# Graph attention with residual and layer norm: ScalarE's work in a step ordered by need, and steps between the load, the codes and the maxima of an edge list

## The chip, the cores and the metric

The kernel runs on one core of a Trainium2 chip. The time is that of the device for one execution, in microseconds (us). The engines are TensorE (PE in the profile, its weight loads PEld), VectorE (DVE), ScalarE (ACT), GpSimd (POOL) and SyncE (SP), which issues most of the DMAs. Each engine works through its own instructions in the order in which they were written, and waits for other engines by semaphores.

## The reference

```python
def ref(x, adj, Wq, bq, Wk, bk, Wv, bv, Wo, bo):      # x: (16, 1024, 512), adj: (1024, 1024) of 0 and 1
    q, k, v = ((x @ W + b).reshape(16, 1024, 8, 64) for W, b in ((Wq, bq), (Wk, bk), (Wv, bv)))
    scores = einsum('bqhd,bkhd->bhqk', q, k) / 8 + (1 - adj) * -1e9
    out = einsum('bhqk,bkhd->bqhd', softmax(scores), v).reshape(16, 1024, 512)
    return layernorm(x + out @ Wo + bo)
```

All in float32. The adjacency is the same for all 16 batch entries and sparse: the chance of an edge falls with the numbers of its two nodes, so the first rows have many edges and the last few.

## The kernel before

The scores of absent edges vanish in the softmax, so the kernel works on edges alone. The 1024 queries of a batch entry are 8 tiles of 128. For each tile, `edges(t)` makes lists from the adjacency once, before or beside the first batch entry. A tile's edges are then worked off in *blocks*: a block gives each of the 128 partitions one edge. `OWN[t]` blocks hold edges of the partition's own query; what queries have beyond that is spread over `BLOCKS[t]` more blocks, whose results are added up by a product with a 0/1 matrix. That is 36 blocks per batch entry, 576 in all.

One *step* n of the main loop does one piece of several blocks: `gather(n + 8)` fetches rows of k and v (and of q) by an indirect DMA on POOL; `products(n + 4)` and `scores(n + 4)` on DVE form q k for 8 heads; `exponentials(n + 3)` on ACT (L720); `weigh(n + 1)` multiplies v by the exponentials, called p v here, either in one DVE operation (L734) or in eight ACT operations, one per head (L730; `by_act` says which); then `add_own(n)` (DVE, L746) adds p v to the tile's sum, or `add_up(n)` does it by two products on PE (L755, L756). When a tile's blocks are through, `normalise` divides by the denominators (DVE, L762 to L769), PE transposes, and `finish` multiplies by Wo, adds x (DVE, L641) and takes the layer norm: the sum of squares on ACT (L648, behind `centre` on DVE, L644), a small root on POOL (L651 to L653), the scaled output on ACT (L656) and its store on SP (L657).

Beside this, PE makes q, k and v of a later batch entry, in units that fill the step up to a share of time: x is transposed (`pxT`, copied to `xT` by ACT, L434), q = x Wq (`pq`, L459; evicted by DVE, L486), and k and v of two tiles at once from seven block products with sums of x and of the weights (`x`, `p6`, `p7`, `z`, `p4`; L575), evicted by ACT (`e`, L588; `kv`, L492) and DVE (L591 to L607). PE's results lie in 4 PSUM banks of the tag `fill` and a few of their own. For a bound on the scores, `norm` squares each q and k (L471, eight ACT operations per tile, one per head, each with a read-out of its accumulator).

The order is written out by hand: the program is recorded step by step, and every engine keeps that order. `later(k, fn)` puts a piece of work into the plan of step n + k. In a step, ACT gets first the exponentials, then the plan's pieces in the order in which they were put there (copies from PSUM, squares, L648, L656), then p v:

```python
                for fn in plan.pop(n, ()):
                    fn()
                if 0 <= n + 1 < total and by_act(n + 1):
                    weigh(n + 1)
```

There are 34 steps before step 0 (n from -34). In them the weights are loaded (`loads`, one piece per step up to each `yield`), the first k and v are made, and the edge lists are begun: `edges(t)` starts in step `EDGES_FROM[t]`. It loads 128 rows of the adjacency (`a`, DMA on SP, L330), multiplies them by column numbers on POOL (`codes`, L332), and one step later sums and checks `a` on ACT (L339 to L341) and begins to take the eight largest codes at a time on DVE (L343, L345). `a`, `codes` and the k and v tiles share 5 buffers of the tag `kv`.

Of the kernel before, what the change touches and what calls it, by code (L numbers as in the profile page):

```python
# [13 lines left out]
OP = mybir.AluOpType  # L14
# [19 lines left out]
ROWS = 3  # L34
EARLY = 10
LEAD_IN = 34
EDGES_FROM = (-32, -16, -12, -8, -4, 0, 5, 10)

PRODUCT = 0.86
SUM = 0.87  # L40
# [3 lines left out]
P = 128  # L44
# [103 lines left out]
def kernel(  # L148
# [34 lines left out]
    nc = tc.nc  # L183
    B, N, D = x.shape
# [26 lines left out]
    def load_w(t, w):  # L211
        nc.scalar.dma_start(t, w.rearrange("(c p) e -> p c e", p=P))

    with ExitStack() as main:
# [16 lines left out]
        place = one.tile([P, N], F32, name="place")  # L231
# [30 lines left out]
        def loads():  # L262

            load_w(W["q"], wq)
            broadcast(bq_bc, bq)
            nc.vector.tensor_scalar(bq_bc, bq_bc, scale, None, op0=OP.mult)
            yield

            B12[0] = work.tile([P, 2, D], F32, tag="kv", name="b12", bufs=5)
            load_w(B11, wk[0:HD2, :])  # L270
            load_w(B21, wk[HD2:D, :])
            load_w(B12[0], wv[0:HD2, :])
            load_w(B22, wv[HD2:D, :])
            yield
            load_w(W["o"], wo)
            yield
            nc.vector.tensor_tensor(T1, B12[0], B11, op=OP.subtract)
            yield
            nc.vector.tensor_tensor(T2, B22, T1, op=OP.subtract)
            nc.vector.tensor_tensor(T3, B22, B12[0], op=OP.subtract)  # L280
            nc.vector.tensor_tensor(T4, B21, T2, op=OP.subtract)
            yield
            nc.vector.tensor_scalar(before, place[:, 0:P], -1.0, query[:, 0:1], op0=OP.add, op1=OP.is_gt)
            yield
            for i in range(ROWS):
                nc.scalar.dma_start(kv_rows[i][N:N + 1, 0:D], zero)
            broadcast(bo_bc, bo)
            yield
            nc.scalar.dma_start(bias_rows[0:NPAIR, :], bq.rearrange("(c p) -> c p", p=P))
            nc.scalar.dma_start(bias_rows[NPAIR:, :], bk.rearrange("(c p) -> c p", p=P))  # L290
            nc.scalar.dma_start(bv_rows, bv.rearrange("(c p) -> c p", p=P))

        def bias_setup():
            bk_bc = work.tile([P, D], F32, tag="y", name="bk_bc", bufs=4)
            broadcast(bk_bc, bk)
            yield
            n8 = small.tile([P, HEADS], F32, name="bk_norms")
            nc.vector.tensor_tensor(bk_bc, bk_bc, bk_bc, op=OP.mult)
            nc.vector.tensor_reduce(n8, bk_bc.rearrange("p (h d) -> p h d", d=HD), axis=AX.X, op=OP.add)
            nc.vector.tensor_reduce(bk_norm, n8, axis=AX.X, op=OP.max)  # L300
            yield
            pb = fill_psum("pb")
            nc.tensor.transpose(pb[:, 0:2 * NPAIR], bias_rows, ident[:2 * NPAIR, :2 * NPAIR])
            nc.tensor.transpose(pb[:, 2 * NPAIR:3 * NPAIR], bv_rows, ident[:NPAIR, :NPAIR])
            yield
            nc.vector.tensor_copy(bias_qk, pb[:, 0:2 * NPAIR])
            bv_col = one.tile([P, NPAIR], F32, name="bv_col")
            nc.vector.tensor_copy(bv_col, pb[:, 2 * NPAIR:3 * NPAIR])
            bvb = work.tile([P, NPAIR, P], F32, tag="y", name="bvb", bufs=4)
            nc.vector.tensor_copy(bvb, bv_col[:, :, None].to_broadcast([P, NPAIR, P]))  # L310
            yield
            pb = fill_psum("pb3")
            for c in range(NPAIR):
                nc.tensor.matmul(pb, bvb[:, c, :], W["o"][:, c, :], start=(c == 0), stop=(c == NPAIR - 1))
            yield
            nc.vector.tensor_tensor(bo_bc, pb, bo_bc, op=OP.add)

        now, plan, urgent = [0], {}, []  # L320

        def later(k, fn):
            plan.setdefault(now[0] + k, []).append(fn)

        def edges(t):
            nb, J, K = BLOCKS[t], DEGREE[t], OWN[t]
            a = work.tile([P, N], F32, tag="kv", name=f"a_{t}", bufs=5)
            nc.sync.dma_start(a, adj[ds(t * P, P), :])  # L330
            v = work.tile([P, N], F32, tag="kv", name=f"codes_{t}", bufs=5)
            nc.gpsimd.tensor_tensor(v, a, place[:, 0:N], op=OP.mult)  # L332
            st = small.tile([P, 4], F32, name="est")
# [5 lines left out]
            nc.scalar.activation(a, a, AF.Copy, accum_out=deg)  # L339
            nc.scalar.activation(a, a, AF.Square, bias=neg_one, scale=2.0)  # L340
            nc.scalar.activation(a, a, AF.Square, bias=neg_one, accum_out=check[:, t:t + 1])  # L341
            for r in range(J // 8):
                nc.vector.max(out=kl[:, ts(r, 8)], in_=v)  # L343
                if r < J // 8 - 1:
                    nc.vector.scalar_tensor_tensor(  # L345
                        v, v, kl[:, r * 8 + 7:r * 8 + 8], v, op0=OP.is_lt, op1=OP.mult
                    )
                    yield
# [117 lines left out]
        def norm(b, t, i, s):  # L466
            if t == 0 and i == 0:
                NRM[b] = work.tile([P, 2, NT, HEADS], F32, tag="nrm", name=f"nrm_{b}", bufs=2)
            for h in range(HEADS):
                sq = work.tile([P, HD], F32, tag="sq", name=f"sq_{b}_{t}_{i}_{h}", bufs=2)  # L470
                nc.scalar.activation(sq, s[:, ts(h, HD)], AF.Square, accum_out=NRM[b][:, i, t, h:h + 1])  # L471

        def pair(b, j):
# [8 lines left out]
            def out_q(i, p):  # L482

                assert gathered[0] >= NB * (b - ROWS + 1)
                q = work.tile([P, D], F32, tag="q", name=f"q_{b}_{tt[i]}", bufs=2)
                nc.vector.scalar_tensor_tensor(q, p, scale, bq_bc, op0=OP.mult, op1=OP.add)  # L486
                nc.sync.dma_start(q_rows[b % ROWS][ds(tt[i] * P, P), :], q)
                later(1, lambda: norm(b, tt[i], 0, q))

            def out_k(i, p):  # L490
                kv = new_kv(i)
                nc.scalar.copy(kv[:, 0:D], p)  # L492
                later(1, lambda: norm(b, tt[i], 1, kv[:, 0:D]))

            def out_v(i, p):
                nc.scalar.copy(KV[b, tt[i]][:, D:], p)
# [99 lines left out]
            def out_k1():  # L596
                kv = KV[b, tt[1]]
                nc.vector.tensor_tensor(kv[:, 0:D], R["p4"], R["g"], op=OP.add)
                send(1)
                later(1, lambda: norm(b, tt[1], 1, kv[:, 0:D]))  # L600

            def out_v1():
                nc.vector.tensor_tensor(new_kv(1)[:, D:], R["z"], R["g"], op=OP.add)
# [30 lines left out]
        def finish(b, t):  # L634

            def out(p):
                OT.pop((b, t))
                y = Y[b, t]

                st = small.tile([P, 5], F32, name="stats", bufs=6)  # L640
                nc.vector.scalar_tensor_tensor(y, p, 1.0, y, op0=OP.mult, op1=OP.add, accum_out=st[:, 0:1])  # L641

                def centre():
                    nc.vector.tensor_scalar(st[:, 1:2], st[:, 0:1], -1.0 / D, None, op0=OP.mult)  # L644

                def spread():
                    sq = work.tile([P, D], F32, tag="ysq", name=f"ysq_{b}_{t}", bufs=1)
                    nc.scalar.activation(sq, y, AF.Square, bias=st[:, 1:2], accum_out=st[:, 2:3])  # L648

                def root():  # L650
                    nc.gpsimd.tensor_scalar(st[:, 2:3], st[:, 2:3], 1.0 / D, EPS, op0=OP.mult, op1=OP.add)  # L651
                    nc.gpsimd.tensor_tensor(st[:, 3:4], st[:, 2:3], neg_half, op=OP.pow)  # L652
                    nc.gpsimd.tensor_tensor(st[:, 4:5], st[:, 3:4], st[:, 1:2], op=OP.mult)  # L653

                def norm_out():
                    nc.scalar.activation(y, y, AF.Identity, bias=st[:, 4:5], scale=st[:, 3:4])  # L656
                    nc.sync.dma_start(out_ap[b, ds(t * P, P), :], y)  # L657
                    del Y[b, t]

                later(1, centre)  # L660
                later(1, spread)
                later(2, root)
                later(4, norm_out)

            out_ap = out_dram
            return product(f"po_{b}_{t}", lambda: OT[b, t], W["o"], out)


# [53 lines left out]
        def by_act(n):  # L722
            b, t, i = blocks[n]
            return 0 < i < OWN[t] or ((b == B - 1 or i >= OWN[t]) and n % 2 == 0)
# [102 lines left out]
        prep = {}  # L827
        for t in range(NT):
            prep.setdefault(EDGES_FROM[t], []).append(edges(t))
        prep.setdefault(8 - LEAD_IN, []).append(bias_setup())  # L830
        preps = [loads()]
        prep.setdefault((B - 1) * NB, []).append(guard())
        with tc.manual_schedule():
# [9 lines left out]
            for t in range(3):  # L843
                load_x(0, t)
            n = -LEAD_IN
            while n < total or plan or urgent or done or finishing:
                now[0] = n
                if n < 0:
                    share = LEAD_SHARE if n > -LEAD_IN else TRANSPOSE * 1.5
# [19 lines left out]
                    normalise(*blocks[n - 1][:2])  # L869
                for fn in plan.pop(n, ()):  # L870
                    fn()
                if 0 <= n + 1 < total and by_act(n + 1):
                    weigh(n + 1)
                credit += share
                if 0 <= n < total and blocks[n][2] >= OWN[blocks[n][1]]:
                    add_up(n)
# [66 lines left out]
```

## Time and profile before

| | |
|---|---|
| median of 3 runs | 2289.22 us (2287.42 to 2289.9) |
| the profiled execution | 2296.11 us, span of its instructions 2294.3 us |
| mean granted clock of TensorE | 0.969 |
| PE busy | 2100.7 us, 92% of the span |
| DVE busy | 1874.1 us, 82% |
| ACT busy | 1642.8 us, 72% |
| POOL busy | 1286.8 us, 56% |
| 16 DMA engines | 578.00 MB, mean 252 GB/s |

A row of the timeline is: start, duration, engine, line, operation, out<-in, and in brackets the engine's idle time before it and what ended that. A row of waits is: engine, what it was about to do, what it waited for; total us, times, longest. A row of a stretch is: from:to, length, the busy time of PE, PEld, DVE, ACT and POOL with their instructions, the granted clock, the busy share of the DMA engines and GB/s. A row of a group of instructions ends with the number, the busy time, the mean ns of one, and the idle time before them by what ended it. The end of a PE product is modelled, so two products that follow each other overlap in these rows; the distance of their starts is the time that one takes.

### The profile page before, as it was taken

What the parts mean: (1) busy time and instruction counts of PE and PEld (TensorE: products, weight loads), DVE (VectorE), ACT (ScalarE), POOL (GpSimd) and SP (SyncE); (2) the same over time, 40 slices, a digit from 0 to 9 for tenths busy, and PEclk for the clock granted to TensorE, in tenths of its full rate; (3) what the DMA queues carried; (4) which work ended last, traced back from release to release, by engine and by line L of the source; (5) the groups of instructions that cost most, each with busy time, mean ns of one, the idle gap of its engine ahead of it and who ended that gap; (6) DMA issues with size and microseconds to landing.
All of it is one profiled execution on the core that took longest, in us unless ns stands there. A gap on an engine that the chain in (4) does not pass through costs nothing. (4 is left out here: it accounts for less than half of the span.)

```text
span 2294.3 us, 29416 instructions
## 1 busy us (share of the span) xinstructions
PE 2100.7 (92%) x5933; PEld 1033.0 (45%) x5933; DVE 1874.1 (82%) x3596; ACT 1642.8 (72%) x8100; POOL 1286.8 (56%) x1366
## 2 busy tenths in 40 slices
PE   7977888989999999999999999999999999999655
PEld 3433434444444444444454444444444444544322
DVE  5678978778887988879888887888788888978665
ACT  3556667587877778676877867687876878687655
POOL 2034455555656565665656555565656566575673
PEclk9989999999999999999999999999999999999868
DMA  4256868687887878787887878788787878778773
GB/s 170 92 191 207 262 217 284 223 266 269 286 283 249 292 257 293 242 278 253 275 289 269 283 235 283 251 285 283 247 289 246 300 260 287 260 258 279 228 240 114
DMA packets 216716, 578.00 MB, mean 252 GB/s; under 512 B 33727, under 2 KB 33739, under 8 KB 216526
## 3 DMA queue, kind: packets, MB, share of 16 engines
q0 software_dynamic: 102144, 331.89, 45.8%
q1 hardware_dynamic: 111776, 239.16, 28.5%
q10 hardware_dynamic: 2606, 4.99, 0.7%
q14 instruction: 141, 1.16, 0.1%
q8 instruction: 49, 0.80, 0.1%
HBM read 474.75 MB, written 134.26 MB: 265 GB/s over the span
## 5 line engine op out<-in xcount | busy, mean ns | idle before, releaser
L689 POOL DMA_INDIRECT kvg<-kv_rows,key_row x576 | 652.3, 1132 | 656.4 <-ACT pv L720 193.3
L730 ACT ACTIVATE pv<-kvg,pv 128x64 f32<-128x64 f32 x2592 | 651.5, 336 | 0.0
L459 PE MATMUL pq<-wq,xT 128*128 128x512 f32 x1024 | 492.0, 604 | 12.8 <-ACT xT L434 5.6
L459 PE MATMUL po<-wo,oT 128*128 128x512 f32 x1024 | 476.0, 605 | 1.7 <-DVE y L641 1.7
L710 DVE TENSOR_REDUCE s<-qk 128x8 f32<-128x512 f32 x576 | 392.0, 681 | 6.4
L684 POOL DMA_INDIRECT qg<-q_rows,query_row x240 | 269.1, 1121 | 91.2 <-issue 64.3
L746 DVE TENSOR_TENSOR pv<-pv,pv 128x520 f32<-128x520 f32 x208 | 153.4, 738 | 196.1 <-ACT pv L730 182.3
L459 PEld LDWEIGHTS po<-wo,oT 128*128 128x128 f32 x1024 | 197.9, 195 | 227.7 <-issue 209.1
L471 ACT ACTIVATE sq<-q 128x64 f32<-128x64 f32 x1024 | 245.7, 242 | 62.5 <-DVE q L486 50.1
L459 PEld LDWEIGHTS pq<-wq,xT 128*128 128x128 f32 x1024 | 191.9, 194 | 200.3 <-issue 170.1
L706 DVE TENSOR_TENSOR qk<-qt,kvg 128x512 f32<-128x512 f32 x336 | 245.7, 731 | 3.4 <-DMA kvg<-kv_rows,key_row 2.6
L575 PE MATMUL x<-b,xT 128*128 128x512 f32 x504 | 240.5, 600 | 7.4 <-ACT e L588 7.4
L471 ACT ACTIVATE sq<-kv 128x64 f32<-128x64 f32 x1024 | 245.0, 242 | 2.5 <-ACT sq L471 0.9
L720 ACT ACTIVATE pv<-s,absent 128x8 f32<-128x8 f32 x336 | 97.2, 294 | 198.3 <-DVE o L763 124.5
L575 PE MATMUL pp<-t,s 128*128 128x512 f32 x504 | 237.2, 593 | 0.0
L648 ACT ACTIVATE ysq<-y,stats 128x512 f32<-128x512 f32 x128 | 92.1, 720 | 180.7 <-DVE stats L644 163.0
L755 PE MATMUL sum<-pv,sums 128*128 128x256 f32 x480 | 155.7, 407 | 68.8 <-ACT pv L730 45.4
L632 POOL TENSOR_TENSOR y<-y,bo_bc 128x512 f32<-128x512 f32 x128 | 170.0, 1328 | 57.2 <-DMA y<-in_x_dram 56.1
L471 ACT ACTIVATION_READ_ACCUMULATOR sq<-q 128x1 f32 x1024 | 192.9, 188 | 0.0
L471 ACT ACTIVATION_READ_ACCUMULATOR sq<-kv 128x1 f32 x1024 | 192.7, 188 | 0.0
L706 DVE TENSOR_TENSOR qk<-qg,kvg 128x512 f32<-128x512 f32 x240 | 182.1, 759 | 6.1 <-DMA kvg<-kv_rows,key_row 5.9
L734 DVE TENSOR_TENSOR pv<-kvg,pv 128x512 f32<-128x512 f32 x252 | 177.0, 702 | 0.0
(144 smaller groups left out, 2954.8 us busy)
## 6 DMA issues: line engine op xcount, KB each, us to landing
kv_rows<-kv SPq DMA_DIRECT2D x128, 512.0 KB
x<-in_x_dram SPq DMA_DIRECT2D x128, 256.0 KB
q_rows<-q SPq DMA_DIRECT2D x128, 256.0 KB
qt<-q_rows SPq DMA_DIRECT2D x128, 256.0 KB
y<-in_x_dram SPq DMA_DIRECT2D x128, 256.0 KB
out_dram<-y SPq DMA_DIRECT2D x128, 256.0 KB
kvg<-kv_rows,key_row POOLq DMA_INDIRECT x576
a<-in_adj_dram SPq DMA_DIRECT2D x8, 512.0 KB
```

The lines of the kernel that those rows point to most:

```text
L459: nc.tensor.matmul(p, lhs()[:, ts(c, P)], w[:, c, :], start=(c == 0), stop=(c == NPAIR - 1))
L471: nc.scalar.activation(sq, s[:, ts(h, HD)], AF.Square, accum_out=NRM[b][:, i, t, h:h + 1])
L575: nc.tensor.matmul(R[bank], l[:, ts(c, P)], right[:, c, :], start=(first and c == 0), stop=(c == 1), skip_group_check=True,)
L632: later(2, lambda: nc.gpsimd.tensor_tensor(Y[b, t], Y[b, t], bo_bc, op=OP.add))
L684: nc.gpsimd.indirect_dma_start(out=QG[n], out_offset=None, in_=q_rows[b % ROWS], in_offset=bass.IndirectOffsetOnAxis(ap=query_row[:, g:g + ...
L689: nc.gpsimd.indirect_dma_start(out=KG[n], out_offset=None, in_=kv_rows[b % ROWS], in_offset=bass.IndirectOffsetOnAxis(ap=key_row[:, g:g + ...
L706: nc.vector.tensor_tensor(QK[n], q, KG[n][:, 0:D], op=OP.mult)
L710: nc.vector.tensor_reduce(S[n], QK.pop(n).rearrange("p (h d) -> p h d", d=HD), axis=AX.X, op=OP.add)
L730: nc.scalar.activation(pv[:, ts(h, HD)], v[:, ds(D + h * HD, HD)], AF.Copy, scale=pv[:, D + h:D + h + 1])
L734: nc.vector.tensor_tensor(pv[:, 0:D].rearrange("p (h d) -> p h d", d=HD), v[:, D:].rearrange("p (h d) -> p h d", d=HD), pv[:, D:, None].to ...
L746: nc.vector.tensor_tensor(PV[b, t], PV[b, t], pv, op=OP.add)
L755: nc.tensor.matmul(PSUM[b, t][:, 0, 0:HD2], m, pv[:, 0:HD2], **kw)
```

## The change

ACT's work in a step is put in another order. The squares of q and k, L648 and L656 go into a second plan, `rest`, which is emptied at the step's end; p v by ACT stands before it and is that of block n + 2 instead of n + 1. DVE's p v stays at n + 1. In `edges`, three steps lie between the load of `a` and the codes, and one between ACT's sums and the first maxima; `EDGES_FROM` is set for that: all lists but the first are loaded four steps earlier than before, their codes and sums are made one step earlier, and their maxima begin in the same step; the first list is loaded one step earlier, and its codes, sums and maxima come two to three steps later. In `loads` and for `bias_setup` some pieces change their step.

```diff
-EDGES_FROM = (-32, -16, -12, -8, -4, 0, 5, 10)
+EDGES_FROM = (-33, -20, -16, -12, -8, -4, 1, 6)
...
             load_w(B22, wv[HD2:D, :])
-            yield
+            for _ in range(3):
+                yield
             load_w(W["o"], wo)
+            for i in range(ROWS):
+                nc.scalar.dma_start(kv_rows[i][N:N + 1, 0:D], zero)
...
+        def later_last(k, fn):
+            rest.setdefault(now[0] + k, []).append(fn)
...
             nc.sync.dma_start(a, adj[ds(t * P, P), :])
+            for _ in range(3):
+                yield
             v = work.tile([P, N], F32, tag="kv", name=f"codes_{t}", bufs=5)
             nc.gpsimd.tensor_tensor(v, a, place[:, 0:N], op=OP.mult)
...
             nc.scalar.activation(a, a, AF.Square, bias=neg_one, accum_out=check[:, t:t + 1])
+            yield
             for r in range(J // 8):
...
-                later(1, lambda: norm(b, tt[i], 0, q))
+                later_last(1, lambda: norm(b, tt[i], 0, q))
...
-                later(1, spread)
+                later_last(1, spread)
                 later(2, root)
-                later(4, norm_out)
+                later_last(4, norm_out)
...
                 for fn in plan.pop(n, ()):
                     fn()
-                if 0 <= n + 1 < total and by_act(n + 1):
-                    weigh(n + 1)
+                if 0 <= n + 2 < total and by_act(n + 2):
+                    weigh(n + 2)
+                for fn in rest.pop(n, ()):
+                    fn()
```

The two other calls of `norm`, for k, change in the same way. From line 317 on, a line has a number that is 5 to 8 higher after the change (L720 becomes L726, L730 L736, L755 L761).

What this moves on ACT in the steady steps, here in steps 236 and 237, which begin with the exponentials of blocks 239 and 240 (tiles are named with their numbers: `pv_238` is p v of block 238, `sq_7_6_0_0` the square of head 0 of q in tile 6 of batch entry 7, `sq_7_6_1_0` that of k; seven more follow each). Before:

```order
L720 ACTIVATE pv_239_10779<-s_239_10756 128x8
L471 ACTIVATE sq_7_6_0_0_10790,nrm_7_9765<-q_7_6_10763 128x64
...
L492 COPY kv_7_6_10806<-x_7_3_10698 128x512
L720 ACTIVATE pv_240_10817<-s_240_10788,absent_107 128x8
L656 ACTIVATE y_5_6_10161<-y_5_6_10161,stats_10686 128x512
L471 ACTIVATE sq_7_6_1_0_10837,nrm_7_9765<-kv_7_6_10806 128x64
...
L730 ACTIVATE pv_238_10745<-kvg_238_10562,pv_238_10745 128x64 x8
```

After, on the same engine:

```order
L726 ACTIVATE pv_239_10779<-s_239_10764 128x8
L498 COPY kv_7_6_10790<-x_7_3_10706 128x512
L736 ACTIVATE pv_238_10753<-kvg_238_10562,pv_238_10753 128x64 x8
L477 ACTIVATE sq_7_6_0_0_10802,nrm_7_9773<-q_7_6_10771 128x64
...
L726 ACTIVATE pv_240_10825<-s_240_10788,absent_107 128x8
L662 ACTIVATE y_5_6_10169<-y_5_6_10169,stats_10694 128x512
L477 ACTIVATE sq_7_6_1_0_10845,nrm_7_9773<-kv_7_6_10790 128x64
```

The p v of block 238 has moved from behind the second step's squares to the first step, behind its copy and ahead of both sets of squares.

On SP, where the first k and v of batch entry 1 are stored (`mean_0` is the row of entry 0 that the first gathers wait for). Before:

```order
L330 DMA a_3_922<-in_adj_dram 128x1024
L487 DMA q_rows_1_114<-q_1_0_929 128x512
L524 DMA kv_rows_0_110<-mean_0_1001 1x512
L423 DMA x_1_5_1008<-in_x_dram 128x512
L423 DMA x_1_6_1012<-in_x_dram 128x512
L678 DMA qt_0_0_1027<-q_rows_0_113 128x512
L487 DMA q_rows_1_114<-q_1_1_1082 128x512
L501 DMA kv_rows_1_111<-kv_1_1_1014 128x1024
L501 DMA kv_rows_1_111<-kv_1_0_932 128x1024
L330 DMA a_4_1098<-in_adj_dram 128x1024
```

After, on the same queue:

```order
L333 DMA a_4_932<-in_adj_dram 128x1024
L493 DMA q_rows_1_114<-q_1_0_934 128x512
L530 DMA kv_rows_0_110<-mean_0_970 1x512
L429 DMA x_1_5_977<-in_x_dram 128x512
L429 DMA x_1_6_981<-in_x_dram 128x512
L684 DMA qt_0_0_1029<-q_rows_0_113 128x512
L493 DMA q_rows_1_114<-q_1_1_1089 128x512
L507 DMA kv_rows_1_111<-kv_1_1_983 128x1024
L507 DMA kv_rows_1_111<-kv_1_0_937 128x1024
L333 DMA a_5_1108<-in_adj_dram 128x1024
```

The load of `a_4` has moved from behind these eight DMAs to the place ahead of them, where `a_3` was; its codes on POOL stand behind four gathers of block rows, as before behind five.

On ACT at the start, around the first edge list (`a_0`) and the copies of x^T. Before:

```order
L471 ACTIVATE sq_0_0_0_7_206,nrm_0_191<-q_0_0_175 128x64
L339 ACTIVATE a_0_184,est_188<-a_0_184 128x1024
L340 ACTIVATE a_0_184<-a_0_184,neg_one_84 128x1024
L341 ACTIVATE a_0_184,check_108<-a_0_184,neg_one_84 128x1024
L471 ACTIVATE sq_0_1_0_0_231,nrm_0_191<-q_0_1_208 128x64
...
L434 COPY xT_0_2_247<-pxT_0_2_211 128x512
L434 COPY xT_0_3_251<-pxT_0_3_216 128x512
L492 COPY kv_0_0_273<-pk_0_221 128x512
```

After:

```order
L477 ACTIVATE sq_0_0_0_7_203,nrm_0_188<-q_0_0_177 128x64
L440 COPY xT_0_2_219<-pxT_0_2_205 128x512
L440 COPY xT_0_3_223<-pxT_0_3_210 128x512
L477 ACTIVATE sq_0_1_0_0_227,nrm_0_188<-q_0_1_185 128x64
...
L498 COPY kv_0_0_266<-pk_0_215 128x512
L344 ACTIVATE a_0_175,est_255<-a_0_175 128x1024
```

The copies of x^T have moved ahead of the three operations on `a_0`.

The order on PE, DVE and POOL is that of before, tile for tile, but for the pieces of the edge lists and of the bias set-up. On SP the stores of the output stand a few places later within their step.

More of the change, by code (lines that the diff above doesn't have):

```diff
@@ L273, in loads @@
             load_w(B22, wv[HD2:D, :])
-            yield
+            for _ in range(3):
+                yield
             load_w(W["o"], wo)
+            for i in range(ROWS):
+                nc.scalar.dma_start(kv_rows[i][N:N + 1, 0:D], zero)
+            nc.vector.tensor_scalar(before, place[:, 0:P], -1.0, query[:, 0:1], op0=OP.add, op1=OP.is_gt)
             yield
@@ L282, in loads @@
             yield
[L283 to L286, printed above, removed]
             broadcast(bo_bc, bo)
-            yield
             nc.scalar.dma_start(bias_rows[0:NPAIR, :], bq.rearrange("(c p) -> c p", p=P))
@@ L316, in bias_setup @@
             nc.vector.tensor_tensor(bo_bc, pb, bo_bc, op=OP.add)
-        now, plan, urgent = [0], {}, []
+        now, plan, rest, urgent = [0], {}, {}, []
         def later(k, fn):
             plan.setdefault(now[0] + k, []).append(fn)
+        def later_last(k, fn):
+            rest.setdefault(now[0] + k, []).append(fn)
         def edges(t):
@@ L341, in edges @@
             nc.scalar.activation(a, a, AF.Square, bias=neg_one, accum_out=check[:, t:t + 1])
+            yield
             for r in range(J // 8):
@@ L492, in out_k @@
                 nc.scalar.copy(kv[:, 0:D], p)
-                later(1, lambda: norm(b, tt[i], 1, kv[:, 0:D]))
+                later_last(1, lambda: norm(b, tt[i], 1, kv[:, 0:D]))
             def out_v(i, p):
@@ L599, in out_k1 @@
                 send(1)
-                later(1, lambda: norm(b, tt[1], 1, kv[:, 0:D]))
+                later_last(1, lambda: norm(b, tt[1], 1, kv[:, 0:D]))
             def out_v1():
@@ L829 @@
             prep.setdefault(EDGES_FROM[t], []).append(edges(t))
-        prep.setdefault(8 - LEAD_IN, []).append(bias_setup())
+        prep.setdefault(12 - LEAD_IN, []).append(bias_setup())
         preps = [loads()]
@@ L845 @@
             n = -LEAD_IN
-            while n < total or plan or urgent or done or finishing:
+            while n < total or plan or rest or urgent or done or finishing:
                 now[0] = n
```

## The prediction

> **What bounds the kernel now.** I read the busy times of the page, then the same in three stretches (the edge lists beside the first steps, the steady steps, the end), then the waits of TensorE (PE) in each stretch, then the timeline of ScalarE (ACT) at one of these waits.
>
> ```profile
> PE 2100.7 (92%) x5933; PEld 1033.0 (45%) x5933; DVE 1874.1 (82%) x3596; ACT 1642.8 (72%) x8100; POOL 1286.8 (56%) x1366
> 100.00:500.00 400.00, 335.86 (x923) 161.24 (x922) 320.73 (x679) 267.77 (x1318) 199.01 (x194) 0.94 0.70 228
> 500.00:2050.00 1550.00, 1506.79 (x4340) 745.28 (x4339) 1321.56 (x2485) 1184.43 (x5937) 927.94 (x982) 1.00 0.81 272
> 2050.00:2295.00 245.00, 171.53 (x444) 85.68 (x444) 172.09 (x342) 148.34 (x624) 145.14 (x168) 0.84 0.65 213
> ```
>
> The first number behind a stretch's length is PE's busy time; the third-last column is the granted clock. From 500 to 2050 us PE is busy 97% and nobody else above 85%: PE is the bound, and only its stalls can be won. From 100 to 500 us VectorE (DVE) is nearly as full as PE (320.7 against 335.9 of 400), and at the end no engine is full: there a chain of short waits sets the pace.
>
> ```profile
> PE sum L755 <- ACT pv L730: 17.1, 19, 2.7
> PE sum L756 <- ACT pv L730: 11.1, 44, 0.3
> DVE pv L746 <- ACT pv L730: 123.5, 90, 3.9
> ACT ysq L648 <- DVE stats L644: 98.1, 66, 3.9
> ACT pv L720 <- DVE s L710: 97.9, 65, 3.7
> ACT pv L720 <- DVE o L763: 82.3, 39, 5.1
> ```
>
> These are waits from 500 to 2050 us (total, times, longest). What PE waits for there is one thing, the p v that ACT makes (L730); DVE waits for the same 123.5 us. ACT is not short of time: it waits itself, 98.1 us for DVE before the squares of a finished tile (L648), with the p v behind them in its queue. The timeline of one such wait, ACT's rows and PE's:
>
> ```profile
> 1050.33 0.20 ACT L720 ACTIVATE pv<-s 128x8 f32<-128x8 f32 x1
> ...
> 1052.91 0.25 ACT L471 ACTIVATE sq<-q 128x64 f32<-128x64 f32 x1
> ...
> 1054.38 0.19 PEld L459 LDWEIGHTS po<-wo,oT 128*128 128x128 f32 x1 [0.24 <-issue]
> 1054.81 0.19 PEld L459 LDWEIGHTS po<-wo,oT 128*128 128x128 f32 x1 [0.24 <-issue]
> ...
> 1056.98 0.80 ACT L656 ACTIVATE y<-y,stats 128x512 f32<-128x512 f32 x1
> 1057.69 0.24 ACT L471 ACTIVATE sq<-kv 128x64 f32<-128x64 f32 x1
> ...
> 1059.60 2.01 ACT L730 ACTIVATE pv<-kvg,pv 128x64 f32<-128x64 f32 x8
> 1060.70 0.70 PE L755 MATMUL sum<-pv,sums 128*128 128x256 f32 x2 [0.99 <-ACT pv L730]
> 1061.65 0.71 PE L756 MATMUL sum<-pv,sums 128*128 128x264 f32 x2 [0.26 <-ACT pv L730]
> ```
>
> Sixteen squares with their read-outs (0.24 us each, 3.8 together) and an output scaling of 0.80 stand ahead of the p v of block 238, whose exponentials were done at 1050.5, and PE starts its first half when four of eight heads are done, its second 0.95 later. The weight loads of 128x512 products follow each other by 0.43 us.
>
> A stall costs more than itself:
>
> ```profile
> 1003.00:1010.50 7.50, 4.50 (x14) 1.97 (x13) 5.08 (x11) 7.27 (x43) 6.48 (x8) 1.00 0.68 214
> 1010.50:1013.90 3.40, 3.40 (x6) 1.31 (x5) 3.37 (x7) 2.64 (x21) 2.41 (x3) 0.50 0.90 292
> ```
>
> PE idles 3.0 of the first 7.5 us, and then gets half its clock for 3.4 us, in which six matmuls start. Such a dip costs 1.7 us.
>
> **The change, part by part.** The sum is made against the profiled execution: 2296.1 us, of which 2294.3 is the span. The median of the runs is 2289.2, 6.9 lower; I take that off at the end.
>
> *p v two steps ahead, squares last (500 to 2050 us).* Nothing is added or removed: ACT's 1643 us stay. A p v by ACT gets a whole step more (the 350 rows of L755 below are 175 sums of the 240 in 576 steps, so some 420 steps in 1550 us: 3.7 us each), and stands ahead of the squares and of L648 and L656 instead of behind them. The longest waits of PE and DVE for it are 2.7 and 3.9 us, so one step covers nearly all. Lower end of the gain: 28.2 us (17.1 + 11.1). The rows of idle time understate it, since a product row is modelled longer than its place: 592 ns mean against 0.43, so 0.16 more for each of the 63 waits, 10 us.
>
> ```profile
> L459 PE MATMUL po<-wo,oT 128*128 128x512 f32 x768 | 348.7, 592 | 0.0
> L756 PEld LDWEIGHTS sum<-pv,sums 128*128 128x128 f32 x350 | 62.2, 190 | 38.6 <-ACT pv L730 31.6 <-issue 0.7
> L755 PEld LDWEIGHTS sum<-pv,sums 128*128 128x128 f32 x350 | 62.0, 189 | 114.5 <-issue 55.5 <-ACT pv L730 47.6 <-DVE qk L706 4.1
> ```
>
> Upper end: 79 us, what the weight loads of the sums wait for ACT (31.6 + 47.6), which includes time in which PE still worked. I take 28 + 10, near the lower end since PE's own rows are the direct ones, less 4 for waits that come up next (DVE's results for PE), plus 7 for the four dips of the clock in this stretch: 41. Copies from PSUM stand in front of the same step's squares, but still behind those of the step before; I give that nothing. [...]
>
> Squares last means L648 and L656 later by one p v (2.0 us). Behind them wait POOL's L651 to L653, on its in-order queue the gathers, and on SP's queue the output store with the loads behind it. The gathers are 8 steps ahead and land in time now (8.5 us of waits in the whole run, below), and a p v that is done a step earlier frees its gather buffer a step earlier. Cost taken: 0; bounds 0 and 128 tiles x 2.0 = 256 us if all of it came through.
>
> *Start (0 to 100 us).*
>
> ```profile
> PE pv L547 <- ACT xT L434: 5.7, 1, 5.7
> 25.78 1.06 ACT L339 ACTIVATE a<-a 128x1024 f32<-128x1024 f32 x1 [8.20 <-POOL codes L332]
> 30.90:37.70 6.80, 5.89 (x7) 2.52 (x8) 6.70 (x10) 6.15 (x40) 0.00 (x0) 0.50 0.13 29
> ```
>
> ACT waits 8.2 us for the codes of the first edge list, with the copies of x^T behind it that PE needs; then the clock is halved for 6.8. With the list three steps later both copies stand ahead of it: 5.7 + 3.4, less 1 for the first products that share the DMA with an earlier load: 8 (bounds 0 and 9). Moving wo's load and the zero rows by two or three steps costs nothing: wo is first used when a first tile is finished, long after.
>
> *Edge lists (100 to 500 us).*
>
> ```profile
> POOL codes L332 <- DMA a<-in_adj_dram: 46.9, 5, 13.3
> DVE kl L343 <- POOL codes L332: 20.2, 4, 6.8
> PE pxT L430 <- DVE q L486: 13.2, 2, 11.7
> PE sum L755 <- ACT pv L730: 12.5, 5, 4.3
> PE x L575 <- ACT e L588: 6.8, 4, 3.5
> PE poT L774 <- DVE query_row L404: 6.5, 1, 6.5
> 150.00:250.00 100.00, 70.76 (x192) 34.72 (x191) 84.22 (x205) 68.74 (x329) 47.98 (x37) 0.85 0.65 206
> ```
>
> POOL waits for the load that was issued in the same step (46.9 us, five times), DVE's maxima wait for POOL, and DVE's results for PE behind the maxima: the 11.7 and the 6.5. With three steps (over 10 us) between load and codes these go. Sum: three quarters of 13.2 and 6.5 (15), half of 6.8 (3), 85% of the p v waits (12.5, with the modelled ends 14: 12), and half of the 24 us that the clock withheld (6% of 400, most of it in the stretch shown here): 42. [...]
>
> ```profile
> 107.88 2.35 POOL L332 TENSOR_TENSOR codes<-a,place 128x1024 f32<-128x1024 f32 x1 [13.34 <-DMA a<-in_adj_dram]
> 108.64 1.59 DVE L370 TENSOR_TENSOR est<-est 128x1 f32<-128x1 f32 x1
> 146.64 0.15 DVE L370 TENSOR_TENSOR est<-est 128x1 f32<-128x1 f32 x1
> ```
>
> Now DVE mostly waits while the codes are made; then it will be at work, and lose up to 2.3 us at each of seven. I take 5 of these 16: the term is 37. Bounds: -16, and 79, what DVE's 320.7 us of work leave of 400. [...]
>
> *End (2050 us on).*
>
> ```profile
> DVE pv L746 <- ACT pv L730: 23.8, 12, 3.9
> POOL stats L651 <- ACT ysq L648: 23.4, 6, 7.0
> DVE qk L706 <- DMA kvg<-kv_rows,key_row: 8.5, 3, 4.5
> ```
>
> (The third row is of the whole run.) The chain here runs through p v and through the squares of y in turn. p v earlier can win at most 23.8; squares behind it can lose 2.0 at each tile that ends there, for 16 of them 32. ACT waits for its squares' input anyway, so I take a gain of 6.
>
> Sum: 41 + 8 + 37 + 6 = 92. 2296.1 - 92 = 2204; less 6.9: **2197 us**, 4.0% faster.
>
> **The rivals.** *Only part comes (2244).* The new p v still stands behind the next exponentials, which wait for DVE up to 5.1 us (L763), longer than a step. If that, or DVE's lateness, takes over half of the steady gain and half of the lists', and the end gives nothing: 8 + 19 + 18 = 45. For it: the 97.9 and 82.3 us above; against it: DVE's own 123.5 us of waits go at the same time.
>
> *More comes (2150).* With stalls gone DVE and ACT run ahead, all dips go, and the lists come near their bound: 60 + 9 + 60 + 10 = 139. For it: the 24 us of the clock alone; against: DVE at 84 of 100 us there.
>
> *Nothing (2289).* p v is issued earlier but ends no earlier, since ACT reaches it no sooner. Against it: in the rows shown ACT had the exponentials 9 us before it began the p v.
>
> *Slower (above 2294).* The squares of y end later, POOL's in-order queue stands at L651, and gathers and y come late. Per tile up to 2.0 us; the 92 us are eaten from 0.72 us per tile on, over 128 tiles. For it: the 23.4 us at the end; against it: POOL waits there only six times, and gathers lead by eight steps.
>
> **How the numbers follow.** Forecast as above, 2170 to 2228: 0.60. Only part: 0.19. More: 0.11. Nothing: 0.03. Slower: 0.07. A range from 2150 to 2252 holds the first, most of the second and half of the third, 0.82. A measurement of this kernel tells changes above about 0.2% (4.6 us) from none. Faster: 0.60 + 0.19 + 0.11 = 0.90; same 0.03; slower 0.07.
>
> **What would show it.** From 500 to 2050 us PE's two rows of waits for ACT's p v below 8 us together, DVE's below 40, PE above 98% busy, no dip of the clock; POOL's waits for the adjacency below 10 us; the 11.7 us wait of PE gone; ACT's busy time unchanged within 5. [...] The prediction fails if PE gets new waits for DVE's q, kv or y of more than 20 us, or if POOL's wait at L651 grows past 100 us.

## The result and the profile after

The changed kernel takes 2136.77 us (median of 4 runs, 2135.87 to 2139.02) against 2289.52 for the kernel before: 152.7 us less, a ratio of 0.9336 with a 95% interval of 0.932 to 0.9352. The forecast was 2197, and the range ended at 2150: the direction was right, the size far too small. The profiled execution took 2136.1 us, with a span of 2133.6.

TensorE has the same 5933 matmul rows in both kernels, from number 228 on (counted from 0) in the same order, so the span can be cut at the same row in both: at numbers 228, 1149 and 5489, which start at 100, 499.8 and 2051.7 us of the kernel before. First the stages of the kernel before, then of the changed one (busy time and count of PE, PEld, DVE, ACT and POOL, then the granted clock):

```profile
0.00:100.00 100.00, 86.49 (x228) 40.75 (x229) 59.74 (x92) 42.22 (x223) 14.66 (x23) 0.97 0.40 137
100.00:499.80 399.80, 335.66 (x922) 161.07 (x921) 320.53 (x679) 267.71 (x1317) 198.98 (x193) 0.94 0.70 228
499.80:2051.70 1551.90, 1506.99 (x4341) 745.45 (x4339) 1322.30 (x2487) 1186.20 (x5944) 928.27 (x983) 1.00 0.81 271
2051.70:2294.30 242.60, 171.53 (x444) 85.68 (x444) 171.55 (x342) 146.64 (x617) 144.85 (x168) 0.84 0.65 214
```

```profile
0.00:89.20 89.20, 81.68 (x228) 39.41 (x229) 63.35 (x101) 42.59 (x224) 16.62 (x24) 1.00 0.46 160
89.20:429.90 340.70, 318.85 (x922) 162.39 (x921) 317.21 (x669) 267.08 (x1325) 194.36 (x193) 0.96 0.78 265
429.90:1903.20 1473.30, 1473.30 (x4341) 751.29 (x4340) 1330.32 (x2493) 1174.81 (x5916) 922.88 (x983) 1.00 0.83 286
1903.20:2133.60 230.40, 161.66 (x445) 83.68 (x443) 165.65 (x336) 148.09 (x639) 148.52 (x168) 0.86 0.69 228
```

The start became 10.8 us shorter, the edge lists 59.1, the steady steps 78.6 and the end 12.2: 160.7 together, the difference of the two spans. In the steady steps PE is now busy without a gap for 1473.3 us. The 4341 rows had shown 45 us of idle time there, yet 78.6 went.

From 429.9 to 1903.2 us PE has no row of waits at all, and VectorE's wait for the p v of ScalarE has shrunk from 123.5 us to this:

```profile
DVE pv L752 <- ACT pv L736: 9.0, 7, 2.2
DVE y L647 <- POOL y L638: 22.6, 14, 4.0
```

ScalarE's timeline of some steps shows the new order: the copies from PSUM, the p v, and only then the output scaling and the squares of y.

```profile
1000.29 0.19 ACT L726 ACTIVATE pv<-s 128x8 f32<-128x8 f32 x1
1000.39 0.57 ACT L784 COPY oT<-poT 128x512 f32<-128x512 f32 x1
1000.86 1.06 ACT L440 COPY xT<-pxT 128x512 f32<-128x512 f32 x2
1001.81 2.02 ACT L736 ACTIVATE pv<-kvg,pv 128x64 f32<-128x64 f32 x8
1003.73 0.30 ACT L726 ACTIVATE pv<-s,absent 128x8 f32<-128x8 f32 x1
1003.92 0.81 ACT L662 ACTIVATE y<-y,stats 128x512 f32<-128x512 f32 x1
1004.63 0.72 ACT L654 ACTIVATE ysq<-y,stats 128x512 f32<-128x512 f32 x1
```

What PE still waits for is in the edge lists (the first three rows, 89.2 to 429.9 us) and at the end; there the largest wait of VectorE is an old one that has grown (the fourth row, 1903.2 us on; 20.9 us before):

```profile
PE pxT L436 <- DVE q L492: 8.1, 2, 4.6
PE sum L761 <- DVE pv L740: 6.7, 1, 6.7
PE poff L371 <- DVE est L368: 4.8, 1, 4.8
DVE y L647 <- POOL y L638: 34.4, 10, 5.4
```

### The profile page after: what moved, and what is told of

It is laid out like the page before. It is cut to its first block, busy times and chain, and to the rows that moved or that the text cites. A ratio compares the mean times of both kernels' runs of the same rounds, so it can differ in the third digit from the quotient of the medians.

```text
span 2133.6 us, 29514 instructions
## 1 busy us (share of the span) xinstructions
PE 2035.5 (95%) x5933; PEld 1036.8 (49%) x5933; DVE 1876.5 (88%) x3596; ACT 1632.6 (77%) x8100; POOL 1282.4 (60%) x1366
## 5 line engine op out<-in xcount | busy, mean ns | idle before, releaser
L736 ACT ACTIVATE pv<-kvg,pv 128x64 f32<-128x64 f32 x2592 | 652.6, 338 | 0.0
L465 PE MATMUL pq<-wq,xT 128*128 128x512 f32 x1024 | 482.8, 595 | 0.0
L638 POOL TENSOR_TENSOR y<-y,bo_bc 128x512 f32<-128x512 f32 x128 | 175.3, 1370 | 179.7 <-DMA y<-in_x_dram 178.9
L712 DVE TENSOR_TENSOR qk<-qt,kvg 128x512 f32<-128x512 f32 x336 | 241.1, 718 | 0.2 <-DMA qt<-q_rows 0.2
L726 ACT ACTIVATE pv<-s,absent 128x8 f32<-128x8 f32 x336 | 96.7, 293 | 150.4 <-DVE o L769 84.7
L740 DVE TENSOR_TENSOR pv<-kvg,pv 128x512 f32<-128x512 f32 x252 | 182.0, 722 | 0.0
L761 PE MATMUL sum<-pv,sums 128*128 128x256 f32 x480 | 146.7, 388 | 26.9 <-DVE pv L740 20.0
L647 DVE SCALAR_TENSOR_TENSOR y<-po,y 128x512 f32<-128x512 f32 x128 | 87.3, 682 | 77.6 <-POOL y L638 64.4
```

What stands on the lines that cost most here:

```text
L465: nc.tensor.matmul(p, lhs()[:, ts(c, P)], w[:, c, :], start=(c == 0), stop=(c == NPAIR - 1))
L638: later(2, lambda: nc.gpsimd.tensor_tensor(Y[b, t], Y[b, t], bo_bc, op=OP.add))
L712: nc.vector.tensor_tensor(QK[n], q, KG[n][:, 0:D], op=OP.mult)
L736: nc.scalar.activation(pv[:, ts(h, HD)], v[:, ds(D + h * HD, HD)], AF.Copy, scale=pv[:, D + h:D + h + 1])
L740: nc.vector.tensor_tensor(pv[:, 0:D].rearrange("p (h d) -> p h d", d=HD), v[:, D:].rearrange("p (h d) -> p h d", d=HD), pv[:, D:, None].to ...
L761: nc.tensor.matmul(PSUM[b, t][:, 0, 0:HD2], m, pv[:, 0:HD2], **kw)
```

## The experiments

Gains by stage are read from the profiled execution of each kernel, cut at the same matmul row, against the 2294.3 us of the kernel before. The change has four runs, each experiment five or six. A ratio is to the kernel before as timed beside it; medians of different groups of experiments come from different chips, on which the kernel before took 2288.0 to 2290.3 us.

| kernel | median us | ratio, 95% interval | start | lists | steady | end |
|---|---|---|---|---|---|---|
| the change | 2136.8 | 0.9336 (0.932 to 0.9352) | 10.8 | 59.1 | 78.6 | 12.2 |
| order only | 2156.0 | 0.9413 (0.940 to 0.9425) | 2.4 | 49.2 | 78.4 | 10.4 |
| lists only | 2271.9 | 0.9916 (0.9903 to 0.9929) | 10.6 | 9.7 | 3.9 | 0.4 |
| p v ahead, squares first | 2153.3 | 0.9401 (0.9389 to 0.9413) | 10.4 | 48.6 | 71.7 | 13.2 |
| squares last, p v not ahead | 2163.0 | 0.9445 (0.9432 to 0.9457) | 11.1 | 53.5 | 62.0 | 6.6 |
| y's squares first | 2142.2 | 0.9355 (0.934 to 0.9369) | 10.0 | 57.1 | 74.3 | 14.7 |
| y addition on VectorE | 2127.2 | 0.9285 (0.9271 to 0.9299) | 10.4 | 59.4 | 78.6 | 18.2 |
| more p v on ScalarE | 2131.2 | 0.9304 (0.9291 to 0.9318) | 11.2 | 64.5 | 78.0 | 11.4 |
| both | 2125.3 | 0.9285 (0.9272 to 0.9298) | 9.6 | 64.2 | 78.5 | 18.4 |
| y three ahead | 2125.3 | 0.929 (0.9277 to 0.9303) | 10.7 | 64.5 | 78.6 | 21.9 |
| warm | 2128.8 | 0.9299 (0.9287 to 0.9312) | 9.9 | 63.2 | 78.6 | 14.0 |

**1. ScalarE's order alone.** The edits to `EDGES_FROM`, `edges`, `loads` and the start of `bias_setup` are undone; the list `rest` and `weigh(n + 2)` stay.

> ScalarE's new order alone (p v two steps ahead, squares and output scaling last), with the edge lists and the loads as before. Theory A (the whole steady loss of TensorE, 83 us by the spacing of its starts, hangs on ScalarE's order): 500 to 2050 us of before become 1471 +-5 us, the start gains nothing, the lists about half of the 59 us that the change gave them (30), the end 12: 2169 us (2160 to 2180). Rival B (the steady steps gain because the edge lists finish earlier and the engines enter the steady part with a lead): the steady gain is below 40 us and the time above 2200 us.

2156.0 us, 13 faster than expected and below theory A's range. The steady stage is 1473.4 us, the changed kernel's to 0.1, so theory A holds for it, and it needs no lead from the edge lists. The lists gained 49.2 where I had expected 30. GpSimd still waits for the adjacency here, longer than in the kernel before (59.7 us in the whole run there):

```profile
448.30:1921.70 1473.40, 1473.40 (x4341) 751.19 (x4340) 1333.82 (x2493) 1174.65 (x5916) 922.79 (x983) 1.00 0.83 286
POOL codes L335 <- DMA a<-in_adj_dram: 73.4, 7, 13.3
PE pxT L433 <- DVE q L489: 15.0, 2, 11.5
```

Those 73.4 us lay beside other work; of PE's waits, the one of 11.5 us for q is the largest that stayed.

**2. The edge lists and loads alone.** The complement: `later` in place of `later_last`, and `weigh(n + 1)` as the last of a step.

> The edge lists with steps between load, codes and maxima and the new order of loads alone; ScalarE's order as before. Theory A: start 10.8 us, lists 25 to 30 us, steady part and end within 5 us of before: 2252 us (2245 to 2260). Rival B: a steady gain of over 30 us here too, 2220 us or less.

2271.9 us, 20 slower than theory A said and outside its range. The steady part stayed as expected (1548.0 us), so rival B falls. The start gained its 10.6, the lists only 9.7. With the 49.2 of the first experiment that makes 58.9 of 59.1, so the two parts add. PE's waits for p v are still there:

```profile
479.50:2027.50 1548.00, 1503.03 (x4341) 743.02 (x4339) 1325.39 (x2487) 1185.36 (x5944) 924.70 (x983) 1.00 0.81 272
PE sum L761 <- ACT pv L736: 21.2, 24, 2.7
PE sum L762 <- ACT pv L736: 11.4, 45, 0.3
PE sum L761 <- ACT pv L736: 12.3, 7, 4.3
PE pxT L436 <- DVE q L492: 9.3, 2, 7.0
```

The second and third rows are of the steady part, the last two of the lists. The wait for q fell from 13.2 to 9.3, that for the p v from 12.5 to 12.3.

**3 and 4. The two halves of the order.** The first of these kernels is the changed one with everything in `plan` again:

```diff
-                later_last(1, lambda: norm(b, tt[i], 0, q))
+                later(1, lambda: norm(b, tt[i], 0, q))
...
-                later_last(1, spread)
+                later(1, spread)
-                later_last(4, norm_out)
+                later(4, norm_out)
```

The second keeps `rest`, but weighs one step ahead:

```diff
-                if 0 <= n + 2 < total and by_act(n + 2):
-                    weigh(n + 2)
+                if 0 <= n + 1 < total and by_act(n + 1):
+                    weigh(n + 1)
                 for fn in rest.pop(n, ()):
                     fn()
```

> The changed kernel with the squares, the squares of y and the output scaling back ahead of the p v in a step; the p v stays two steps ahead. Theory A1 (one more step of lead, 3.3 us, covers all that can stand ahead of a p v; the place of the squares gives nothing): 2137 to 2147 us, TensorE's waits for p v in the steady part below 5 us together. Rival A2 (the squares ahead of the p v are the cause, the step of lead is an extra): above 2165 us.

> The changed kernel with the p v at one step ahead as before, but the squares and the output scaling behind it. Theory A1: the p v still stands behind copies from PSUM and behind exponentials that wait for VectorE, so about a third of the steady loss stays (25 us): 2165 us (2155 to 2180). Rival A2: within 6 us of the changed kernel, 2137 to 2143 us.

The first takes 2153.3 us, between A1 and A2, with PE's waits for p v as small as A1 said; the second takes 2163.0, as A1 said, though only 16.6 us of steady loss stay where it had 25. In the steady part either half alone takes most of the 78.6 us: 71.7 and 62.0. They do not add, since they remove the same lateness: with the squares and the output scaling out of the way a p v is in time for most sums, and with a step of lead it is in time although they stand before it. In the edge lists the squares in front cost the first kernel another 10.5 us. What the squares in front still cost in the steady part shows as single waits elsewhere (y), and what one step leaves short, as a wait for p v and for oT:

```profile
440.80:1921.00 1480.20, 1476.97 (x4342) 749.95 (x4341) 1322.59 (x2494) 1176.34 (x5928) 922.48 (x984) 1.00 0.83 285
PE pxT L436 <- DVE y L647: 1.0, 1, 1.0
PE sum L762 <- ACT pv L736: 0.5, 2, 0.3
435.30:1925.20 1489.90, 1481.13 (x4342) 748.38 (x4340) 1337.99 (x2490) 1176.15 (x5929) 931.38 (x984) 1.00 0.83 282
PE po L465 <- ACT oT L784: 2.3, 3, 0.9
PE sum L762 <- ACT pv L736: 1.8, 7, 0.3
```

(First the p v ahead, from the fourth row on the squares last.) These idle rows add up to 3.2 and 8.8 us, while the stages are 6.9 and 16.6 us longer than the changed kernel's: again PE's idle rows show about half of what is lost.

**5. Squares of y and output scaling ahead of the p v again.** `later` for `spread` and `norm_out` alone, to price the rival that makes the kernel slower.

> The changed kernel with the squares of y and the output scaling back ahead of the p v in a step; the squares of q and k stay last. It prices the prediction's rival that squares of y behind the p v make GpSimd's in-order queue, and with it gathers and y, late: GpSimd waits 76 us for these squares in the changed kernel against 25.5 before. Theory A (these waits lie beside other work): 2133 to 2141 us, as the changed kernel. Rival C (they cost up to 2 us at each of the 16 tiles of the end): faster than the changed kernel by 10 to 30 us, the gain lying in the last 230 us.

2142.2 us, 5.4 above the changed kernel's median, with intervals that overlap: not faster. The end is 2.5 us shorter, so the squares of y behind the p v do cost something there, far from 10 to 30, and the steady part is 4.3 longer. Rival C falls. The waits that it rested on did grow in the changed kernel, from 25.5 us in 8 waits:

```profile
POOL stats L657 <- ACT ysq L654: 76.1, 35, 7.8
```

**6. The addition for y on VectorE at the end.** In the changed kernel VectorE stands 4 to 5 us at each tile near 2000 us, with GpSimd busy 28.7 of the 36 us from 1996 on, with gathers and the small roots among it, which its program puts before the addition. The edit:

```diff
-            later(2, lambda: nc.gpsimd.tensor_tensor(Y[b, t], Y[b, t], bo_bc, op=OP.add))
+            adder = nc.gpsimd if fronts else nc.vector
+            later(2, lambda: adder.tensor_tensor(Y[b, t], Y[b, t], bo_bc, op=OP.add))
```

> The changed kernel with the addition of the bias to y on VectorE instead of GpSimd for the tiles that are loaded after the set-up work has run out (the last 190 us). Theory D (the end is set by GpSimd's queue: the addition of 1.27 us stands behind gathers there, and VectorE waits 34.4 us for it in 10 waits, TensorE behind VectorE): the end stage becomes 20 us shorter, 2117 us (2107 to 2127). Rival E (the end is a chain of short waits: VectorE then waits for the load of y or TensorE for the next thing): 2133 to 2141 us.

2127.2 us: the end gained 6.0 us in the profile and the medians differ by 9.6, a third to a half of what D said. The 34.4 us went, and two other waits came, as rival E had it:

```profile
DVE y L648 <- PE po L465: 12.7, 5, 4.0
DVE y L639 <- DMA y<-in_x_dram: 11.9, 7, 2.8
```

**7. Ten more p v of batch 0 on ScalarE.**

```diff
-            return 0 < i < OWN[t] or ((b == B - 1 or i >= OWN[t]) and n % 2 == 0)
+            return 0 < i < OWN[t] or ((b in (0, B - 1) or i >= OWN[t]) and n % 2 == 0) or (b == 0 and n % 4 == 1)
```

> The changed kernel with ten more of the 36 p v of batch 0 on ScalarE, taken from VectorE, which is 93% busy from 100 to 500 us. Theory F (what is left in the edge-list stage, 38 us, is VectorE's lateness and the clock behind it): VectorE loses 6.8 us of work there, the stage becomes 5 to 12 us shorter, 2128 us (2122 to 2133). Rival G (ScalarE, with 20 us more in that stage, makes its p v late again): 2137 us or more.

2131.2 us, and the lists 5.4 shorter: theory F, at the lower end. ScalarE had the room.

**8 and 9. Both, and y loaded three tiles ahead** (`done[:3` for `done[:2`, five buffers for y).

> The changed kernel with both edits together: the addition of the bias to y on VectorE for the tiles of the end, and ten more p v of batch 0 on ScalarE. Theory D and F (two stages, so the gains add): 9.6 and 5.6 us, 2122 us (2118 to 2126). Rival: they share a cause and do not add, above 2127 us.

> The kernel of both edits with y tiles loaded three ahead instead of two at the end, and five buffers for them instead of four. With the addition on VectorE that engine waits 11.9 us for these loads. Theory D: these waits go and the end is 5 to 12 us shorter, 2113 us (2108 to 2118). Rival E (the end is a chain of short waits, and TensorE is late for the next reason): within 4 us of the kernel of both edits, 2118 to 2126.

Both together take 2125.3 us. Both gains are in the profile (64.2 and 18.4), but the time does not show that they add: the median lies only 1.9 below that of the sixth kernel, which was timed on another chip, and the ratios to the kernel before are equal (0.9285). The eighth kernel beats the kernel before and the changed one: 0.9285 against 0.9336, with intervals that do not meet. The ninth has a median of 2125.3 and runs from 2120 to 2130: rival E holds and the 5 to 12 us of theory D did not come; whether the earlier loads help by less stays open.

**10. More work for TensorE at the end.** Products that nobody reads, added to the eighth kernel:

```diff
             pv = PV.pop(n)
+            if b == B - 1:
+                p = fill_psum(f"warm_{n}")
+                for _ in range(3):
+                    nc.tensor.matmul(p, ident, pv[:, 0:D], start=True, stop=True)
```

> The kernel of both edits with three more 128x512 products that nobody reads (1.29 us at full clock) for each of the 18 own blocks of the last batch, which have no sums: 23 us more work for TensorE in the stretch where it idles. Theory H (the clock of each stretch of 3.41 us is set by how much of the stretch before TensorE worked, full from about 0.39 on): the half clock of 1994 to 2035 us goes, products of the output take 3.4 us for eight instead of 5.2, and the end becomes up to 10 us shorter: 2116 us (2110 to 2122). Rival I (the clock follows something else, so more work is only more work): the dips stay and the time is 2125 to 2145 us.

2128.8 us. The work added is more than was meant. A batch has 21 own blocks, not 18, and in the trace the 63 products of 512 columns in float32 are 126 rows, for each of which the 429 ns hold that were counted for a whole product. That is 54 us at full clock:

```profile
L753 PE MATMUL warm<-pv,ident x126: 592/592/1062, 2001.9 to 2103.1; 128*128 128x512 f32 x126
```

The clock rose as H says and the gain did not come. Kernel 8 first, then this one:

```profile
1990.00:2110.00 120.00, 77.50 (x197) 41.34 (x196) 92.06 (x195) 76.85 (x280) 71.30 (x90) 0.78 0.67 223
1990.00:2115.00 125.00, 115.15 (x320) 57.28 (x319) 92.64 (x194) 77.29 (x281) 72.05 (x91) 0.97 0.64 215
```

It went from 0.78 to 0.97, but the full clock was spent on the added products, with which PE is busy 92% of the stretch. So half clock at the end was not a cost that could be had back this way. Whether fewer products, which leave PE room, would gain was not tried.

## Why the prediction was wrong in size

**Steady steps: 41 forecast, 78.6 measured; the step that failed.** "I take 28 + 10, near the lower end since PE's own rows are the direct ones" was wrong twice. First, the correction for modelled ends was too small and given to too few waits. PE's true pace is seen in the spacing of its starts where it waits for nothing: 429 ns for a row of 512 columns, 216 and 222 for the rows of a sum's two halves, 109 for one of a transpose. Against that, and with half clock counted apart, the 82 sums whose p v ScalarE makes lose 56.6 us in the steady stage of the kernel before and 0.1 after the change. The rows of waits give 28.2, and the prediction had 38. A sum's row is modelled as 379 ns or more, as the changed kernel shows, and takes 216:

```profile
L761 PE MATMUL sum<-pv,sums x480: 379/379/795, 171.3 to 2112.3; 128*128 128x256 f32 x160
```

Second, beside the waits for p v and the dips of the clock (6.9 us, right) I counted nothing to be won, and took 4 off for new waits. Instead another 20 us went that had been lost in small waits for copies of x^T, for kv, y and e. They left with ScalarE's order, as the first experiment shows. That its late p v made VectorE late too, which waited 123.5 us for them, and VectorE's results for PE with it, fits these figures; no run tests it alone. Together the spacing of starts gives 83 us of loss for that stage before and 4 after. The upper bound in the text, 79 us, agrees with the 78.6 by luck: it adds up what weight loads wait for p v, and the gain is made of 56 at those sums, 7 of clock and 15 of other waits.

**Start: 8 forecast, 10.8 measured.** Right, with the mechanism: the list's codes no longer stand before the copies, no dip of the clock is left before 133 us, and of the 10.8 the second experiment, without the new order, keeps 10.6.

**Edge lists: 37 forecast, 59.1 measured; the same step failed.** GpSimd's waits for the adjacency, the waits of PE behind them and the 5 us for rows of VectorE beside the codes make 15 - 5 = 10 in the sum. They are the lists' part of the change, and the second experiment gives 9.7 for it. That agreement is in part luck: PE's wait for q was to fall by three quarters and fell from 13.2 to 9.3 there, and a new one for est came (4.8 in the changed kernel). The other terms of the sum, 12 for p v, 3 for e and 12 of clock, are 27 where ScalarE's order alone gained 49.2. By spacing this is 22 at the sums whose p v ScalarE makes, 7 behind e, 8 of clock, and 13 at the transposes of the output and the products with Wq and Wo, less 7 of new waits for VectorE's p v and est. Here too the p v was mis-sized and the waits further on were left out. No run shows the 5 or the 16 of that term: beside the eight codes VectorE's rows last 5.0 us longer than their medians before and 7.1 after, 2.1 more. One such row has one small tensor as input; it takes 2.56 us and ends as the codes do (161.05 against 161.01 us), and the next row of that form (L408) takes 0.17:

```profile
158.49 2.56 DVE L407 TENSOR_SCALAR ee<-ee 128x2 f32<-128x2 f32 x1
161.08 0.17 DVE L408 TENSOR_SCALAR ee<-ee 128x2 f32<-128x2 f32 x1
...
158.66 2.35 POOL L337 TENSOR_TENSOR codes<-a,place 128x1024 f32<-128x1024 f32 x1
```

**End: 6 forecast, 12.2 measured.** The gain of an earlier p v came; the loss by later squares of y is the 2.5 us of experiment 5. The next thing late is y's addition on GpSimd, which the prediction did not name.

**The rivals.** "More comes" had the right signs and a chance of 0.11, but its terms stopped at 60 of 79 in both stages although nothing in the profile held back the rest: ScalarE and VectorE were 76% and 85% busy in the steady part. Its 10 for the end with the upper bounds of the other three parts (79, 9 and 79) would have given 2112, and the range should have reached toward it. "Only part" (exponentials that wait for VectorE) is answered by the first two rows of the next fence: ScalarE's waits for VectorE did not grow but shrank (97.9 and 82.3 us before), with VectorE's own wait for p v nearly gone.

```profile
ACT pv L726 <- DVE s L716: 83.3, 38, 5.0
ACT pv L726 <- DVE o L769: 48.7, 22, 4.1
POOL codes L337 <- DMA a<-in_adj_dram: 5.0, 1, 5.0
```

**The signs listed.** Held: PE's waits for p v (none), VectorE's (9.0), PE above 98% (100), no dip in the steady part, GpSimd's wait for the adjacency below 10 us (the third row). Neither sign of failure came: PE's waits for q and y stay below 10 us each in the whole run, and GpSimd's at L657 are 76.1 us for the squares and 14.8 for another row of ScalarE, near the 100 that was named. Missed: the wait of 11.7 us for q is 4.6, not gone; ScalarE's busy time fell by 10.2 us, not within 5. Its groups kept their durations (652.6 for the p v against 651.5); its instructions that overlap in the trace do so by about 0.1 us (median 0.095 before, 0.096 after), and its gaps of over 0.15 us fell from 370 to 251.

**The 6.9 us between profile and median** did not recur: the profiled execution of the changed kernel is 0.7 below its median. So 160 us of difference in the profiles are 152.7 in the medians, and taking them off was no error.

## What to carry to other kernels

Where an in-order engine is late and not full, order its work by who waits for it, and judge the gain by the spacing of the bound engine's starts against the spacing without waits, since busy time and idle rows showed little more than half of it here. A lead of one step and moving the unhurried work back are two cures for the same lateness: either took 62 to 72 of 79 us, both together all of it. If the other engines have room (76% and 85% busy in the steady part here), put the whole loss by spacing into the upper end of the range: here 79 of 83 us went.

## What the runs showed of the hardware

In the traces of the kernel before and of the changed one, all dips of TensorE's clock to half start on a grid of 3413 ns, and last whole numbers of it (but for a last one that ends with the trace): in the kernel before 3.41 us at 1010.51, 17.07 at 2184.69. For each stretch of the grid I took the share that TensorE's matmul rows would fill at their full-clock spacing (429 ns for 512 columns, as above), in the 1240 stretches of both traces from 90 us on. Above 0.39 the next stretch was at full clock every time, below 0.34 at half clock every time, and between them both occur. So in these traces the clock was halved behind a stretch with some 2.1 us of idle time, about 0.6 of it, whether in one piece (2.17 us, before the dip at 184.48 in the kernel before) or several (four, the longest 1.47 us, 2.09 together, before that at 1010.51). Where a stall falls in the grid counts: in the kernel before, 3.41 us from 962.0 on, across two stretches, were filled to 0.32 and no dip followed; the two stretches were filled to 0.92 and 0.40. Nor did it take an idle stretch: of the 66 stretches at half clock, 43 follow one in which TensorE's rows fill more than a twentieth. Experiment 10 tests it from the other side: with work in the gaps the clock from 1990 us on was 0.97, against 0.78 without.
